# One core, two layers: where an image's tables are made, how a scan starts, and how a layer's beginning is cut up

## The chip, the core and the metric

The kernel runs on one core of a Trainium2 chip. The core has five engines with instruction queues of their own: TensorE (PE in the profile; PEld is its weight load), VectorE (DVE), ScalarE (ACT), GpSimd (POOL) and SyncE (SP), which here only issues DMAs. Each engine works through its queue in order and waits on semaphores for the others. The metric is the device time of one execution in microseconds (us), the median of several.

## The reference

The input `x` has 4 images of 128 x 128 pixels with 128 channels in float32. Two layers follow one another, each on a group-normalized input and each with a residual sum:

```
x = x + L0(gn(x))     # deformable convolution: per pixel 9 offsets, bilinear samples, depthwise 3x3, pointwise
x = x + L1(gn(x))     # two Mamba blocks over each image row (128 tokens)
```

What matters of the first layer is its sampling, from four neighbours of a fractional place:

```
out = wa * gather(y0, x0) + wb * gather(y1, x0) + wc * gather(y0, x1) + wd * gather(y1, x1)
```

and of the second, its selective scan, whose state has 16 numbers for each of 256 inner channels:

```
delta  = softplus(dt @ dtw + dtb)
h      = exp(delta * A) * h + (delta * u) * B      # one token after another
y      = sum over states of h * C   (+ u * D)
```

## The kernel before

**First layer (`layer0(b)`).** A work item is a unit `(j, u)`: four image rows `j` of 32 (`NJ`), and one of nine pairs of taps (`UNITS`). `gather` (L353) issues eight indirect DMAs per unit on POOL; each fetches, for 128 pixels by an index each, one row of a table in DRAM. The table of an image is made by `table_part(b, j)` (L207) from the normalized image, four rows at a time. Its row `e` has 2 x 128 numbers: for the pixel and for its neighbour to the right, the 64 channels of the pixel and of the one below it. So one index brings all four neighbours (1024 B). DVE normalizes (`xt` times `row_s`, plus `row_b`), SP issues eight writes a part: two channel groups, the pixel and its right neighbour, the upper and the lower row. Ahead of it, `stats_part(b, j)` (L181) loads four rows, transposes them on PE and takes their statistics on DVE, and `norm_part(b)` makes scale and bias of an image. `sample` (L373) multiplies what was gathered by the weights (`gw`, L382, on DVE), adds it up transposed on PE (`p`), and copies it with ACT to `s`; `add_up` (L399) runs the depthwise and pointwise products on PE. Gathered tiles have four buffers (`NGT`), two of which are a unit. `prep` makes indices and weights for eight rows.

Within `layer0(b)` stands a list `todo` (L428): the 32 statistics parts, the normalization and the 32 table parts of image `b + 1`, spread over the units of image `b`, three to each four rows. Image 0's own are made ahead of everything.

**Second layer (`layer1`).** A job is four image rows and one of two blocks; there are 256 jobs, 64 for each image, in the order: two row groups through block 0, the same two through block 1. `pre` (L484) begins a job: input products (`pu`, `pr`, L501 and L513), Silu for `u` and `g` on ACT, the small product `pdb` with its copy `dbl`, from which SP stores `bcd` to DRAM, then the softplus for `delta`: Abs, Exp, +1 and Ln on ACT (L538 to L546) and four half operations and two whole ones on DVE (L547 to L550: `e`, `de`, `du`). `main` (L553) has eight steps (`q`), two states each. In a step, SP loads B and C for it spread over all partitions (`bc`, two buffers each), ACT writes `da = exp(delta * A)` in four pieces (L580) into one of three `da` buffers, and DVE runs three operations of 128 x 2048: `hs` (L586, two instructions), the scan (L592), which overwrites `da` with the state, and the product with C (L596). PE then adds the result up transposed in PSUM (`y`, L128). After eight steps DVE multiplies `y` by the gate (`g`, L607), PE transposes and multiplies by the output weights, and ACT copies; in block 1 the result goes out from a tile `ot`.

All products are written as `scalar_tensor_tensor` with a column of `ones` as their scalar; the scan takes its initial value from a column `zero`.

**The order.** The program first makes image 0's statistics and table, then runs `layer0(0)` alone. Then it runs `layer1` over all images, and beside image `b`'s 512 steps the units of `layer0(b + 1)`, spread so that they end 24 steps early. Image 3's second layer has nothing beside it. In `layer1`, `pre` of the next job is written out whole ahead of `main` of the present one. The layer that turns the program into queues moves instructions within each engine's queue, so the built order is not that of the text; ACT's table loads (ACT_TABLE_LOAD) are put in where the function set changes.

Of the kernel before, what the change touches and what calls it, by code (L numbers as in the profile page):

```python
# [10 lines left out]
F32 = mybir.dt.float32  # L11
# [6 lines left out]
P = 128  # L18
G = 2
# [44 lines left out]
def block_kernel(ctx: ExitStack, tc: tile.TileContext, a: dict, out: bass.AP):  # L64
# [71 lines left out]
    dwb = loadw("dwb", [P, NT], pool=p2, tag="ot")  # L136
# [21 lines left out]
    dpar = loadw("dpar", [P, NL, NC], pool=p2, tag="ot")  # L158
# [32 lines left out]
    def norm_part(b):  # L191

        scale, bias = group_norm(nc, small, ps, stats[b], gavg, 1e-5, f"a{b}")
        rows = []
        for nm, v in (("s", scale), ("b", bias)):
            dg = small.tile([P, P], F32, tag="dg", name=f"dg_{nm}_{b}")
            nc.vector.tensor_scalar(dg, ident, v, None, ALU.mult)
            pr = ps.tile([P, 512], F32, tag="t", name=f"prow_{nm}_{b}")
            nc.tensor.matmul(pr[:, 0:P], ones, dg, start=True, stop=True)
            row = small.tile([P, P], F32, tag=f"row_{nm}", name=f"row_{nm}_{b}")  # L200
            nc.scalar.copy(row, pr[:, 0:P])
            rows.append(row)
        norm[b] = (scale, bias, rows[0], rows[1])
# [3 lines left out]
    def table_part(b, j):  # L207
        if j == 0:
            table[b] = dram.tile([G * (H - 1) * W, 2, 2 * CG], F32, name=f"table_{b}")
# [6 lines left out]
        nc.vector.tensor_tensor(xv, xv, brow.unsqueeze(1).to_broadcast([P, n + 1, P]), ALU.add)  # L216
        for g in range(G):

            e0 = (g * (H - 1) + 4 * j) * W
            for sx in range(2):  # L220

                parts = [(0, n, 0)] if e0 or not sx else [(0, 1, 1), (1, n - 1, 0)]
                for r, m, p0 in parts:
                    e = e0 + r * W - sx
                    tv = table[b][e + p0 : e + m * W, sx]
                    if p0 == 0:
                        tv = tv.rearrange("(r w) e -> w r e", w=W)
                    else:
                        tv = tv.unsqueeze(1)
                    for sy in range(2):  # L230
                        nc.sync.dma_start(
                            tv[:, :, CG * sy : CG * sy + CG],
                            xt[p0:, r + sy : r + sy + m, CG * g : CG * g + CG],
                        )
# [118 lines left out]
    def gather(b, j, u):  # L353

        wt, idx = locs[b, j // 2]
        flat = table[b][0 : G * (H - 1) * W - 1].rearrange("n s e -> n (s e)")
# [69 lines left out]
    def layer0(b):  # L426

        todo = []  # L428
        if b + 1 < B:
            todo += [lambda j=j: stats_part(b + 1, j) for j in range(NJ)]  # L430
            todo += [lambda: norm_part(b + 1)]
            todo += [lambda j=j: table_part(b + 1, j) for j in range(NJ)]
# [50 lines left out]

    def pre(st, l):  # L484
# [25 lines left out]
        for i in range(SR // 2):  # L510
# [7 lines left out]
            tc.keep_in_program_order(nc.scalar.activation(g[:, 2 * i : 2 * i + 2], px, AF.Silu))  # L518
        pdb = ps1.tile([P, TB], F32, tag="t", name=f"pdb_{nm}")
# [6 lines left out]
        nc.sync.dma_start(bcd, dbl[DTR + 1 : XP, :])  # L526

# [3 lines left out]
        es, pdts = [], []  # L531
        for c in range(NC):
# [4 lines left out]
            e = p2.tile([P, TB], F32, tag="e", name=f"e_{nm}_{c}", bufs=2)  # L537
            nc.scalar.activation(e, pdt, AF.Abs)  # L538
            nc.scalar.activation(e, e, AF.Exp, scale=-1.0)
            es.append(e)  # L540
            pdts.append(pdt)
        for c in range(NC):
            e = es[c]
            w1 = p2.tile([P, TB], F32, tag="w1", name=f"w1_{nm}_{c}")
            nc.scalar.activation(w1, e, AF.Identity, bias=1.0)
            nc.scalar.activation(du[:, c], w1, AF.Ln)  # L546
            nc.vector.scalar_tensor_tensor(e, w1, 1.0, e, op0=ALU.subtract, op1=ALU.subtract)  # L547
            nc.vector.scalar_tensor_tensor(de[:, c], pdts[c], 0.0, e, op0=ALU.max, op1=ALU.subtract)  # L548
# [4 lines left out]
    def main(st, l):  # L553
# [11 lines left out]
        for q in range(NS // NQ):  # L565
# [10 lines left out]
            for c in range(NC):  # L576
                dv = st["delta"][:, c].rearrange("p (s t) -> p s t", s=SR)
                for n in range(NQ):
# [3 lines left out]
                    )  # L582
            hs = p2.tile([P, NC, NQ, TB], F32, tag="hs", name=f"hs_{nm}_{q}")

            for n in range(NQ):
                nc.vector.scalar_tensor_tensor(  # L586
                    hs[:, :, n, :], st["du"], ones[:, 0:1],
                    bc[0][:, n].unsqueeze(1).to_broadcast([P, NC, TB]),
                    op0=ALU.mult, op1=ALU.mult,
                )  # L590
            df = da.rearrange("p c n s t -> p (c n s t)")
            nc.vector.tensor_tensor_scan(  # L592
                df, df, hs.rearrange("p c n t -> p (c n t)"), zero[:, 0:1], ALU.mult, ALU.add
            )
            dc = da.rearrange("p c n s t -> p c (n s t)")
            nc.vector.scalar_tensor_tensor(  # L596
                dc, dc, ones[:, 0:1],
                bc[1].rearrange("p n t -> p (n t)").unsqueeze(1).to_broadcast([P, NC, NQ * TB]),
                op0=ALU.mult, op1=ALU.mult,
            )  # L600
# [19 lines left out]
        else:  # L620
# [8 lines left out]
            ot = p2.tile([P, SR, P], F32, tag="ot", name=f"ot_{nm}")  # L629
# [11 lines left out]
    def layer1():  # L641
        pre(*jobs[0])
        for i, job in enumerate(jobs):
            if i + 1 < len(jobs):
                pre(*jobs[i + 1])
            yield from main(*job)
# [101 lines left out]
```

## Time and profile before

| what | value |
| --- | --- |
| time, median of 3 runs | 26681.26 us (26681.15 to 26698.94) |
| the profiled execution | 26698.06 us, span 26696.0 us |
| busy: PE / DVE / ACT / POOL | 19620.5 / 23505.8 / 11605.1 / 16017.0 us |
| share of the span: PE / DVE / ACT / POOL | 73 / 88 / 43 / 60% |
| mean granted TensorE clock | 0.845 |
| indirect gathers (POOL) | 9216, mean 1738 ns |
| ACT_TABLE_LOAD before `da` (L580) / before Ln (L546) | 1016 / 500, 1283 ns each |

Busy time is time in which the engine executed an instruction; waits, and the issue of DMAs, are not counted. A group line of the profile names the source line, the engine, the operation, what it writes and reads with shapes, its count, then busy time and the mean of one, and after the second bar how long the engine stood idle just before these instructions and what ended that. A list of waits gives who waited for whom: total us, times, longest. A timeline line has the start, the duration, and in brackets the idle time before it. The 40-slice view gives the busy share in tenths.

### The profile page before, as it was taken

The page shows a single profiled execution, that of the slowest core. Times are in us where ns is not written, and L with a number is a line of the kernel's source. Part 1 is how long each engine was busy: PE and PEld are TensorE (multiplying, and loading weights), DVE is VectorE, ACT ScalarE, POOL GpSimd, SP SyncE. Part 2 cuts the span into 40 slices and gives each one's busy share as a digit, 9 for nine tenths or more (in the row PEclk, how much of TensorE's full clock was granted, in tenths as well). Part 3 has the DMA queues.
Part 4 walks back from the last instruction along what each step waited for, and adds up shares of the span by engine and source line. Part 5 has one row for each costly group of instructions (what it writes and reads, how often), then busy time and mean ns, then how long its engine had stood idle before and what let it go on. Part 6 is the DMA issues. An engine that isn't in the chain of part 4 may idle for free. (4 is left out here: it accounts for less than half of the span.)

```text
span 26696.0 us, 294801 instructions
## 1 busy us (share of the span) xinstructions
PE 19620.5 (73%) x112196; PEld 13523.4 (51%) x112196; DVE 23505.8 (88%) x14042; ACT 11605.1 (43%) x18181; POOL 16017.0 (60%) x9222
## 2 busy tenths in 40 slices
PE   4777788878888778887888778888888655555555
PEld 3444455555555555555555555555555443434344
DVE  2232289999999999999999999999999999999999
ACT  0000044444444544444444454444445455555554
POOL 4777777878877767888878667877878400000000
PEclk7888888888999888888998888899998866666666
DMA  5363344456544444455544444444444333333332
GB/s 146 114 172 107 106 147 155 157 170 183 165 153 154 149 144 155 158 173 181 164 154 153 148 143 151 156 150 152 154 154 156 130 107 106 107 106 107 107 106 102
DMA packets 1994602, 3804.53 MB, mean 143 GB/s; under 512 B 771796, under 2 KB 1116116, under 8 KB 1993053
## 3 DMA queue, kind: packets, MB, share of 16 engines
q1 hardware_dynamic: 1550812, 2577.13, 29.9%
q0 software_dynamic: 442368, 1208.55, 14.4%
q8 instruction: 880, 14.42, 0.2%
q14 instruction: 542, 4.43, 0.0%
HBM read 3567.63 MB, written 217.05 MB: 142 GB/s over the span
## 5 line engine op out<-in xcount | busy, mean ns | idle before, releaser
L364 POOL DMA_INDIRECT gt<-table,idx x9216 | 16016.3, 1738 | 5031.5 <-issue 2999.5
L592 DVE TENSOR_TENSOR_SCAN da<-da,zero,hs 128x2048 f32<-128x2048 f32 x2048 | 9176.1, 4481 | 351.7 <-ACT da L580 247.1
L128 PE MATMUL y<-ident,da 128*128 128x128 f32 x32768 | 5252.0, 326 | 3956.1 <-DVE da L596 3955.4
L580 ACT ACTIVATE da<-de,aneg 128x508 f32<-128x508 f32 x8192 | 5550.5, 712 | 5605.2 <-PE y L128 5351.0
L128 PEld LDWEIGHTS y<-ident,da 128*128 128x128 f32 x32768 | 4682.4, 171 | 4953.3 <-DVE da L596 2520.6
L415 PE MATMUL acc<-s,wc 128*64 128x256 f32 (+3 forms) x38400 | 6403.2, 453 | 761.4 <-ACT s L396 760.9
L586 DVE SCALAR_TENSOR_TENSOR hs<-du,ones,bc 128x1024 f32<-128x1024 f32 x4096 | 5093.2, 1277 | 0.0
L415 PEld LDWEIGHTS acc<-s,wc 128*64 128x64 f32 x38400 | 3352.0, 145 | 3083.2 <-issue 1446.2
L596 DVE SCALAR_TENSOR_TENSOR da<-da,ones,bc 128x2048 f32<-128x2048 f32 x2048 | 4807.9, 2348 | 25.9
L382 DVE TENSOR_TENSOR gw<-gt,wt 128x1024 f32<-128x1024 f32 x2304 | 2786.4, 1213 | 2133.3 <-DMA gt<-table,idx 1500.9
L128 PE MATMUL p<-ident,gw 128*128 128x128 f32 x18432 | 2724.3, 299 | 1714.1 <-DVE gw L382 1706.7
L128 PEld LDWEIGHTS p<-ident,gw 128*128 128x128 f32 x18432 | 2292.8, 154 | 2329.3 <-DVE gw L382 1752.7
L396 ACT COPY s<-p 128x512 f32<-128x512 f32 x1152 | 668.6, 581 | 3989.8 <-PE p L128 3982.0
L501 PE MATMUL pu<-hp,inc 128*128 128x512 f32 x4096 | 1808.3, 593 | 0.0
L580 ACT ACT_TABLE_LOAD x1016 | 1303.5, 1283 | 16.8 <-PE y L128 5.7
L501 PEld LDWEIGHTS pu<-hp,inc 128*128 128x128 f32 x4096 | 751.2, 188 | 865.9 <-issue 865.2
L508 ACT ACTIVATE u<-pu,w_cvb 128x512 f32<-128x512 f32 x512 | 324.6, 684 | 1468.9 <-PE y L561 1461.4
L561 PEld LDWEIGHTS y<-ddiag,u 128*128 128x128 f32 x4096 | 579.5, 200 | 192.0 <-issue 192.0
L612 PE MATMUL pyg<-ident,g 128*128 128x128 f32 x2048 | 353.9, 328 | 425.7 <-DVE g L607 424.8
L546 ACT ACT_TABLE_LOAD x500 | 641.5, 1283 | 8.9
L561 PE MATMUL y<-ddiag,u 128*128 128x128 f32 x4096 | 612.1, 284 | 0.0
L263 PE MATMUL pof<-xn,w_offw 128*64 128x512 f32 x2304 | 585.0, 613 | 20.0 <-ACT xn L257 12.0
(118 smaller groups left out, 11036.3 us busy)
## 6 DMA issues: line engine op xcount, KB each, us to landing
bc<-bcd SPq DMA_DIRECT2D x4096, 512.0 KB
gt<-table,idx POOLq DMA_INDIRECT x9216
table<-xt SPq DMA_DIRECT2D x984, 128.0 KB
xt<-in_x SPq DMA_DIRECT2D x124, 320.0 KB
xr<-in_x SPq DMA_DIRECT2D x128, 256.0 KB
x<-xo SPq DMA_DIRECT2D x128, 256.0 KB
x1t<-x SPq DMA_DIRECT2D x128, 256.0 KB
x1t_o<-x SPq DMA_DIRECT2D x128, 256.0 KB
```

The costliest lines, as they stand in the source:

```text
L128: nc.tensor.matmul(o, v, ident, is_transpose=True, start=start, stop=stop, skip_group_check=True)
L364: nc.gpsimd.indirect_dma_start(out=gt[:, v, r], out_offset=None, in_=flat, in_offset=bass.IndirectOffsetOnAxis(ap=idx[:, ri, o : o + 1], a ...
L382: nc.vector.tensor_tensor(gw.rearrange("p r s v c -> p (r s) v c"), gts[h].rearrange("p v r (s c) -> p (r s) v c", c=CG), wv.unsqueeze(3). ...
L396: nc.scalar.copy(st[:, :, 1 : W + 1], p4)
L415: nc.tensor.matmul(accs[b, j + i0][CG * g : CG * g + CG, q : q + rb - ra, :], wc[sl, v, e, :], st[p + 4 * g if p < 4 else 8][sl, ra:rb, kx ...
L501: nc.tensor.matmul(px.rearrange("p (s t) -> p s t", s=SR), inc[:, l, j, c * P : (c + 1) * P], h[:, :, j : j + P], start=(j == 0), stop=(j ...
L546: nc.scalar.activation(du[:, c], w1, AF.Ln)
L561: nc.tensor.matmul(y[:, i, c], st["u"][:, c, i * P : (i + 1) * P], ddiag[:, l, c, :], start=(i % 2 == 0 and c == 0), stop=False, skip_grou ...
L580: nc.scalar.activation(da[:, c, n, :, 1:], dv[:, :, 1:], AF.Exp, scale=aneg[:, l, c, s : s + 1])
L586: nc.vector.scalar_tensor_tensor(hs[:, :, n, :], st["du"], ones[:, 0:1], bc[0][:, n].unsqueeze(1).to_broadcast([P, NC, TB]), op0=ALU.mult, ...
L592: nc.vector.tensor_tensor_scan(df, df, hs.rearrange("p c n t -> p (c n t)"), zero[:, 0:1], ALU.mult, ALU.add)
L596: nc.vector.scalar_tensor_tensor(dc, dc, ones[:, 0:1], bc[1].rearrange("p n t -> p (n t)").unsqueeze(1).to_broadcast([P, NC, NQ * TB]), op ...
```

## The change

The change has five parts.

1. `todo` is filled in `layer0(0)` alone, with the statistics, normalization and tables of images 1, 2 and 3: 195 items, seven to each four rows, where each `layer0(b)` had 65 for the next image.
2. A table row has half the size: the pixel and the one below it, for 64 channels. One index still fetches 256 numbers, which are now two rows in succession, the pixel and its right neighbour. The sums go into a new tile `xg`, laid out by channel group, with one buffer; SP issues eight writes a part, one for each row and group.
3. The scan's initial value is the constant 0.0.
4. In the last image's jobs `hs` and the product with C are plain `tensor_tensor` operations, `hs` as one instruction in place of two.
5. `pre` is a generator with four stops. `main` advances it once per step, so the next job's beginning is written out in pieces behind the first five steps. In it, the softplus works on whole 128 x 1024 tiles: ACT takes the maximum (Relu) and subtracts 1, and DVE has four whole operations.

Some tiles change their tag, so that the memory suffices: `ot` shares with `w1`, and the diagonal matrices of the normalization share with `wn`.

```diff
     def table_part(b, j):
         if j == 0:
-            table[b] = dram.tile([G * (H - 1) * W, 2, 2 * CG], F32, name=f"table_{b}")
+            table[b] = dram.tile([G * (H - 1) * W, 2 * CG], F32, name=f"table_{b}")
...
         nc.vector.tensor_tensor(xv, xv, srow.unsqueeze(1).to_broadcast([P, n + 1, P]), ALU.mult)
-        nc.vector.tensor_tensor(xv, xv, brow.unsqueeze(1).to_broadcast([P, n + 1, P]), ALU.add)
+
+        xg = pb.tile([P, G, 5, CG], F32, tag="xg", name=f"xg_{b}_{j}", bufs=1)
         for g in range(G):
...
+            c = slice(CG * g, CG * g + CG)
+            nc.vector.tensor_tensor(
+                xg[:, g, 0 : n + 1], xv[:, :, c], brow[:, c].unsqueeze(1).to_broadcast([P, n + 1, CG]), ALU.add
+            )
+        for g in range(G):
             e0 = (g * (H - 1) + 4 * j) * W
...
+            for r in range(n):
+                nc.sync.dma_start(
+                    table[b][e0 + r * W : e0 + r * W + W], xg[:, g, r : r + 2].rearrange("p r c -> p (r c)")
+                )
...
-        flat = table[b][0 : G * (H - 1) * W - 1].rearrange("n s e -> n (s e)")
+
+        flat = table[b][:]
...
-        if b + 1 < B:
-            todo += [lambda j=j: stats_part(b + 1, j) for j in range(NJ)]
-            todo += [lambda: norm_part(b + 1)]
-            todo += [lambda j=j: table_part(b + 1, j) for j in range(NJ)]
+        for i in range(1, B) if b == 0 else ():
+            todo += [lambda i=i, j=j: stats_part(i, j) for j in range(NJ)]
+            todo += [lambda i=i: norm_part(i)]
+            todo += [lambda i=i, j=j: table_part(i, j) for j in range(NJ)]
...
+        yield
         pdb = ps1.tile([P, TB], F32, tag="t", name=f"pdb_{nm}")
...
         nc.sync.dma_start(bcd, dbl[DTR + 1 : XP, :])
+        yield
...
-            nc.scalar.activation(e, pdt, AF.Abs)
-            nc.scalar.activation(e, e, AF.Exp, scale=-1.0)
...
-        for c in range(NC):
-            e = es[c]
-            w1 = p2.tile([P, TB], F32, tag="w1", name=f"w1_{nm}_{c}")
-            nc.scalar.activation(w1, e, AF.Identity, bias=1.0)
-            nc.scalar.activation(du[:, c], w1, AF.Ln)
-            nc.vector.scalar_tensor_tensor(e, w1, 1.0, e, op0=ALU.subtract, op1=ALU.subtract)
-            nc.vector.scalar_tensor_tensor(de[:, c], pdts[c], 0.0, e, op0=ALU.max, op1=ALU.subtract)
+            nc.scalar.activation(e[:, c], pdt, AF.Abs)
+            nc.scalar.activation(de[:, c], pdt, AF.Relu)
+        nc.scalar.activation(e, e, AF.Exp, scale=-1.0)
+        nc.scalar.activation(w1, e, AF.Identity, bias=1.0)
+        nc.scalar.activation(du, w1, AF.Ln)
+        nc.scalar.activation(w1, w1, AF.Identity, bias=-1.0)
+        yield
+        yield
+        nc.vector.tensor_tensor(e, w1, e, ALU.subtract)
+        nc.vector.tensor_tensor(de, de, e, ALU.subtract)
         nc.vector.tensor_tensor(de, de, du, ALU.add)
...
+            if in_last(blk):
+                nc.vector.tensor_tensor(
+                    hs,
+                    st["du"].unsqueeze(2).to_broadcast([P, NC, NQ, TB]),
+                    bc[0].unsqueeze(1).to_broadcast([P, NC, NQ, TB]),
+                    ALU.mult,
                 )
...
-                df, df, hs.rearrange("p c n t -> p (c n t)"), zero[:, 0:1], ALU.mult, ALU.add
-            )
...
+                df, df, hs.rearrange("p c n t -> p (c n t)"), 0.0, ALU.mult, ALU.add
+            )
+            if in_last(blk):
+                nc.vector.tensor_tensor(dc, dc, cv, ALU.mult)
+            else:
+                nc.vector.scalar_tensor_tensor(dc, dc, ones[:, 0:1], cv, op0=ALU.mult, op1=ALU.mult)
...
     def layer1():
-        pre(*jobs[0])
+        for _ in pre(*jobs[0]):
+            pass
         for i, job in enumerate(jobs):
-            if i + 1 < len(jobs):
-                pre(*jobs[i + 1])
-            yield from main(*job)
+
+            nxt = pre(*jobs[i + 1]) if i + 1 < len(jobs) else iter(())
+            for _ in main(*job):
+                next(nxt, None)
+                yield
+            for _ in nxt:
+                pass
```

## The prediction

> **What bounds the kernel now.** I read first the page's 40 slices, then busy time by stage, then the groups of VectorE (DVE), what it waits for, and the timeline of single steps.
>
> ```profile
> PE   4777788878888778887888778888888655555555
> DVE  2232289999999999999999999999999999999999
> POOL 4777777878877767888878667877878400000000
> ...
> 330.00:1330.00 1000.00, 792.90 (x4989) 494.38 (x4989) 276.08 (x315) 76.16 (x133) 773.47 (x744) 0.88 0.39 114
> 1345.00:2345.00 1000.00, 795.70 (x4918) 478.51 (x4914) 309.32 (x368) 75.75 (x135) 774.87 (x740) 0.88 0.55 150
> 2400.00:3400.00 1000.00, 788.10 (x4893) 472.35 (x4893) 257.38 (x280) 76.22 (x134) 772.12 (x749) 0.88 0.36 106
> 3436.00:21354.00 17918.00, 14309.54 (x83937) 9846.38 (x83937) 17474.17 (x10407) 8668.91 (x13655) 13606.18 (x6898) 0.89 0.48 156
> 21354.00:26696.00 5342.00, 2791.45 (x12672) 2140.90 (x12672) 5061.15 (x2489) 2691.71 (x4093) 0.00 (x0) 0.69 0.31 106
> ```
>
> Columns of the stretches: length, then busy time of PE, weight load, DVE, ACT, POOL. There are three stages. To 3436 image 0's first layer runs alone; DVE is a quarter busy, and POOL issues one gather per 1000/749 = 1.335 us without waiting for anything but itself: POOL is the bound. The three stretches there hold image 1's statistics (744 gathers), its table (740) and neither (749). From 3436 to 21354 DVE is 97.5% busy (second layer of images 0 to 2 beside the first layer of images 1 to 3). From 21354 POOL is idle and the second layer of image 3 runs alone: 64 jobs in 5342 us, 83.5 us each, DVE 94.7% busy.
>
> ```profile
> L592 DVE TENSOR_TENSOR_SCAN da<-da,zero,hs 128x2048 f32<-128x2048 f32 x2048 | 9176.1, 4481 | 351.7 <-ACT da L580 247.1 <-PE pdt L534 11.2 <-DVE hs L586 3.3
> L586 DVE SCALAR_TENSOR_TENSOR hs<-du,ones,bc 128x1024 f32<-128x1024 f32 x4096 | 5093.2, 1277 | 0.0
> L596 DVE SCALAR_TENSOR_TENSOR da<-da,ones,bc 128x2048 f32<-128x2048 f32 x2048 | 4807.9, 2348 | 25.9
> L549 DVE TENSOR_TENSOR de<-de,du 128x1024 f32<-128x1024 f32 x256 | 311.3, 1216 | 1.4 <-ACT du L546 1.2
> L607 DVE TENSOR_TENSOR g<-y,g 128x1024 f32<-128x1024 f32 x256 | 310.9, 1214 | 110.1 <-PE y L128 109.7
> L303 DVE TENSOR_TENSOR wn<-loc,fl 128x288 f32<-128x288 f32 x64 | 29.0, 452 | 0.0
> L304 DVE SCALAR_TENSOR_TENSOR wn<-loc,wn 128x288 f32<-128x288 f32 x64 | 28.9, 452 | 0.0
> ...
> 23159.36 4.49 DVE L592 TENSOR_TENSOR_SCAN da<-da,zero,hs 128x2048 f32<-128x2048 f32 x1
> 23163.88 2.35 DVE L596 SCALAR_TENSOR_TENSOR da<-da,ones,bc 128x2048 f32<-128x2048 f32 x1
> 23166.15 2.48 DVE L586 SCALAR_TENSOR_TENSOR hs<-du,ones,bc 128x1024 f32<-128x1024 f32 x2
> 23168.76 4.49 DVE L592 TENSOR_TENSOR_SCAN da<-da,zero,hs 128x2048 f32<-128x2048 f32 x1
> ...
> DVE da L592 <- ACT da L580: 196.3, 62, 5.6
> ```
>
> A step in the last image is three DVE operations back to back, scan to scan 9.40 us. The last row is the last image's one wait of size: 62 times in 64 jobs the scan waits for ACT's `da`. The timeline puts it at the third scan behind a job's start: ACT is then at the next job's beginning, switching tables (1.28 us a load, eight a job) and standing for PE, between the `da` of one step.
>
> **The change, part by part**, summed against the profiled execution, 26698.06 us (2 us more than its span).
>
> *Constant scan initial.* A `[P,1]` operand has a price in these rows: 1277 ns with `ones` against 1216 without at 128x1024, while L304, with a constant for its scalar, takes the 452 of the plain L303. I take the same 0.06 us off each scan. The scan with a constant isn't in the trace: bounds 0 and -0.06. 2048 x 0.06 = **-123 us**, all on DVE; 512 of them are in the last image, 1536 before.
>
> *Plain products in the last image.* 1024 more elements cost 2348 - 1277 = 1071 ns, so a plain product of 2048 takes about 1216 + 1071 = 2287 ns. The pair of `hs` (2.48 us) becomes one of 2.29, the `da` product goes from 2.35 to 2.29: 0.25 x 512 = **-128 us**. POOL, which such products could hold up, does nothing there.
>
> *The delta chain.* Per job DVE has now four half operations (0.60 us from start to start, L547 and L548) and two of 128x1024 (1.12): 4.62 us with the shorter first one. Four of 1.12 are 4.48: 256 x 0.14 = **-36 us**. ACT takes over the maximum (a Relu per half) and the -1 (one pass), some 2 us a job, and drops table loads: 2036 to 1040 in the built order, 996 x 1.283 = 1278 us. ACT is 50% busy in the last image, so this counts only through waits.
>
> *The layer in pieces: waits that go.* In the built order ACT does all four `da` of a step before the next job's first Silu, then both Silu pairs under one load, and Exp and Ln under one load each. By the durations above, the `da` of the third step after a job's start is then done some 10 us ahead of its scan, where it is now up to 5.6 late. So I take out 196 + 11 us (last image), and in the stretch before, the 51 us of the same wait and 20 of L547 for L545: **-278 us**; bounds 0 and that.
>
> *A wait that comes.* `g` (L607) reads the last transposes of the job before, which PE ends 3.83 us after DVE's last product (the trace's last `g` waits so long with nothing in between). Now in the last image scan and `hs` stand ahead of it, and it doesn't wait. In the changed order 47 of 64 times only the one `hs` product (2.2 us) does: 47 x 1.6 = 75 us. Before the last image `g` stands right behind the `hs` pair 117 times where it was 69; at 106 us for 76 waits, 1.4 each, 48 more are 67 us. Behind `g` waits the scan, and all of DVE. **+142 us**; bounds 40 and 180.
>
> *Statistics and tables of images 2 and 3 out of the DVE-bound stretch.* There, 64 statistics (44 us), 128 products and sums of the table (103), small ones (2); less 0.08 us overlap each (15), plus 10 of waiting for PE: **-144 us**. Their DMAs leave too: 64 x (8 table writes + 1 load) and 64 loads on SP. The busy share of DVE is 98.4% between 11000 and 13000, where a table is written, 97.7% between 7000 and 9000, where less is, so I give nothing for them.
>
> *The same work in stage 0.* Seven items per four rows now, not three. A statistics part cost (749 - 744) x 1.335 / 31 = 0.2 us of POOL's pace, a table part (749 - 740) x 1.335 / 31 = 0.4: 64 x 0.2 + 64 x 0.45 = 42 us (the sum is now two operations). A table part issues 8 writes of 64 KB in 512 B rows, where it was 8 of 128 KB in 256 B rows, behind one another on SP with the next part's load, and ahead of image 0's loads; DMA is busy 0.55 there, so bandwidth is no bound. But `xg` has one buffer: the sums of a part wait until the 8 writes of the part before have landed, about 8 x 0.5 + 2 us, and the `gw` products of the gathers stand behind them on DVE. In the built order this falls on every second part; `gw` has about 4 us of waiting for its gather per half unit to hide it in, and four gather buffers keep POOL going. I take 33 us for what isn't hidden: **+75 us**, bounds +20 and +250. Image 0's own table, before any gather, keeps its pace: SP's 16 issues take 9.0 of 14.4 us per two parts now, and the single buffer makes a chain of the same length (within 30 us either way).
>
> The port that both engines need is where a page bears on this.
>
> ```profile
> 12008.06 4.03 POOL L364 DMA_INDIRECT gt<-table,idx  x1 [0.31 <-issue]
> 12006.85 4.47 DVE L592 TENSOR_TENSOR_SCAN da<-da,zero,hs 128x2048 f32<-128x2048 f32 x1
> ```
>
> A gather that takes 0.95 us alone took 4.03 and ended 0.77 us after the scan beside it. The Trainium skill (GPSIMD Engine Reference, § Specifications) says that POOL's path to SBUF contends with DVE instructions that have two SBUF inputs. That speaks against moving tables into the one stage that POOL bounds: by the rule each added table operation could hold a gather for all its length, where the counts above gave 0.4 us a part. It is the second rival.
>
> **Sum**: -123 - 128 - 36 - 278 + 142 - 144 + 75 = -492, so 26,206 for an execution like the profiled one. The median shown, 26,681.26, lies 17 us lower; I predict **26,200 us**.
>
> **Rivals.**
>
> 1. *A gather becomes two rows: slower.* The table's row is now 512 B, and one index fetches 1024 B, two rows. If POOL wrote a descriptor per table row, its 0.95 us would double at most: stage 0 alone gets 2304 x 0.95 = 2190 us longer, 28,400; the point from which it decides is 492 / 2304 = 0.21 us per gather. For it: no gather in the trace fetches past its row. Against: the destination stays one run of 1024 B, and the built instruction names 256 elements per index as before. Chance 0.07.
> 2. *POOL held in full.* 64 parts x (0.81 + 2 x 0.48) of table operations hold gathers for their whole length: 113 us, 84 more than my 29: 26,290. For it the 4.03 us above; against it the count of gathers. 0.07.
> 3. *The pieces free nothing.* The waits for `da` move to another step, because Relu and the -1 come into the same queue: 278 stay, 26,480. For it: PE's order puts the products of the next job's beginning ahead of the transposes; against: eight loads become four. 0.10.
> 4. *Single `xg`.* If DVE's standing on the writes reaches POOL at each of 96 parts with 2.5 us: +240 in place of 33, 26,410. For it: every part's sums wait on all 8 writes; against: four gather buffers. 0.08.
> 5. *Gains and losses cancel* within 0.2%, some 53 us, about what a measurement of this kernel tells from no change. 0.04.
>
> **How the numbers follow.** The forecast has 0.64. It, POOL held, the pieces and `xg` all end faster: 0.89. Same 0.04, slower 0.07. Range: best, with +20 in stage 0, +40 for `g` and 30 off the first table, the sum is -679, so 26,019; I take 26,030, since the ends hardly all come together. Above, 26,450 holds all of rivals 2 and 4 and nearly reaches 3. The forecast's own range is 26,060 to 26,340.
>
> **What would show it.** Scan 4.42 us; last image: one `hs` product of 2.29, scan to scan 9.07, a job about 79.5; `da` from ACT gone from DVE's waits there, `g` for PE come in its place with about 1.6 us each; DVE's stretch before it shorter by some 300 us; stage 0 ending near 3510 in place of 3436, with POOL's gathers at 1.37 to 1.39 us apart. Gathers above 1.5 us would be rival 1; `xg` waiting for table DMAs beside POOL waiting for `gw` would be rival 4.

## The result, and the profile after

The changed kernel takes **26059.91 us** (median of 4 runs, 26054.35 to 26064.71) where the kernel before takes 26685.15 on the same chip: a ratio of 0.9765, 95% interval 0.9748 to 0.9782, or 625 us less. The prediction said 26,200 with a range of 26,030 to 26,450. It lies inside, 140 us too high.

The groups of the profile after that answer to those shown of before, from the page (line, engine, operation, tiles and count, then busy time, mean ns of one, idle time before):

```profile
L603 DVE TENSOR_TENSOR_SCAN da<-da,hs 128x2048 f32<-128x2048 f32 x2048 | 9049.6, 4419 | 108.4 <-DVE hs L597 2.3
L607 DVE TENSOR_TENSOR da<-da,bc 128x2048 f32<-128x2048 f32 x512 | 1172.6, 2290 | 14.3
L587 DVE TENSOR_TENSOR hs<-du,bc 128x2048 f32<-128x2048 f32 x512 | 1169.5, 2284 | 0.0
```

A scan with a constant initial takes 4419 ns where it took 4481; the plain products take 2284 and 2290 ns; ACT's `da` no longer stands among what the scan waits for. The working's unit prices for these three are confirmed to the hundredth of a microsecond. A job of the last image takes 79.3 us (5075.5 / 64, from 20980.9 on) where some 79.5 were forecast.

To see where the time came from, I cut both executions at two instants that are easy to find in any of these traces: the start of the first scan (the end of stage 0) and the start of the last product with gathered data (`gw`, the end of the first layers).

| kernel | first gather | stage 0 (to the first scan) | middle | last part | span |
| --- | --- | --- | --- | --- | --- |
| before | 319.7 | 3471.2 | 17594.2 | 5630.6 | 26696.0 |
| changed | 275.7 | 3429.0 | 17265.7 | 5361.7 | 26056.4 |
| difference | -44.0 | -42.2 | -328.5 | -268.9 | -639.6 |
| the prediction's terms | 0 | +75 | -267 | -300 | -492 |

The last row sorts the terms on record by stage: middle 1536 x 0.06 + 192 x 0.14 + 71 - 67 + 144 = 267, last part 31 + 128 + 9 + 207 - 75 = 300. The terms took the last image for the last part, which holds some 3.5 jobs more. So two stages came out near their sums, one 61 better and one 31 worse, and stage 0 came out 117 better.

The same cut in busy time by stretch (length; then PE, weight load, DVE, ACT, POOL):

```profile
3429.00:20694.70 17265.70, 13940.06 (x82728) 9563.39 (x82724) 16947.89 (x9650) 7820.08 (x12659) 13573.22 (x6880) 0.89 0.47 154
20694.70:26056.00 5361.30, 2978.07 (x13475) 2258.89 (x13473) 5196.26 (x1996) 2589.43 (x4061) 0.00 (x0) 0.70 0.33 111
```

DVE is 98.2% busy in the middle and 96.9% in the last part: it remains the bound, and what is left idle is 318 and 165 us. Half of the latter is one kind of wait. The last image's waits of DVE, and the timeline around one of them:

```profile
DVE g L616 <- PE y L128: 78.8, 48, 3.8
DVE e L547 <- ACT w L544: 10.1, 36, 0.3
```

```profile
23109.42 4.42 DVE L603 TENSOR_TENSOR_SCAN da<-da,hs 128x2048 f32<-128x2048 f32 x1
23113.88 2.29 DVE L607 TENSOR_TENSOR da<-da,bc 128x2048 f32<-128x2048 f32 x1
23116.08 2.29 DVE L587 TENSOR_TENSOR hs<-du,bc 128x2048 f32<-128x2048 f32 x1
23119.99 1.23 DVE L616 TENSOR_TENSOR g<-y,g 128x1024 f32<-128x1024 f32 x1 [1.62 <-PE y L128]
23121.14 4.41 DVE L603 TENSOR_TENSOR_SCAN da<-da,hs 128x2048 f32<-128x2048 f32 x1
```

The `da` wait of before (196.3 us, 62 times) is gone entirely. In its place `g` waits 48 times for PE's transposes, 1.6 us each: the last product of a job (L607) ends at 23116.17, only one `hs` stands between, and `g` is next in the queue before PE is done. Behind it waits the scan.

In stage 0 the chain is POOL's. Its gathers keep their pace: 1040 ns each from the first gather to the end of the stage in both kernels, and that stretch is 3151 us before and 3153 after although 128 more items run beside it. What DVE waits for between the first gather and the end of the stage, before and after:

```profile
DVE gw L382 <- DMA gt<-table,idx: 1388.8, 393, 16.7
DVE gw L382 <- PE p L128: 604.3, 113, 15.6
```

```profile
DVE gw L377 <- DMA gt<-table,idx: 1388.2, 408, 11.3
DVE gw L377 <- PE p L128: 272.1, 64, 7.4
DVE xg L220 <- DMA table<-xg: 167.5, 46, 6.5
```

DVE does wait for `xg`'s writes, as rival 4 had it, but that doesn't lengthen the stage: `gw` waiting for PE falls from 604.3 to 272.1 us.

### The profile page after: what moved, and what is told of

Same layout as the page of the kernel before. It is cut to its first block, busy times and chain, and to the rows that moved or that the text cites. A ratio compares the mean times of both kernels' runs of the same rounds, so it can differ in the third digit from the quotient of the medians.

```text
span 26056.4 us, 293200 instructions
## 1 busy us (share of the span) xinstructions
PE 19489.8 (75%) x112196; PEld 13423.5 (52%) x112196; DVE 23278.6 (89%) x13146; ACT 10677.0 (41%) x17185; POOL 16003.4 (61%) x9222
## 5 line engine op out<-in xcount | busy, mean ns | idle before, releaser
L603 DVE TENSOR_TENSOR_SCAN da<-da,hs 128x2048 f32<-128x2048 f32 x2048 | 9049.6, 4419 | 108.4 <-DVE hs L597 2.3
L410 PE MATMUL acc<-s,wc 128*64 128x256 f32 (+3 forms) x38400 | 6153.9, 446 | 346.9 <-ACT s L391 345.1
L597 DVE SCALAR_TENSOR_TENSOR hs<-du,ones,bc 128x1024 f32<-128x1024 f32 x3072 | 3829.9, 1280 | 0.0
L609 DVE SCALAR_TENSOR_TENSOR da<-da,ones,bc 128x2048 f32<-128x2048 f32 x1536 | 3605.0, 2347 | 18.2
L607 DVE TENSOR_TENSOR da<-da,bc 128x2048 f32<-128x2048 f32 x512 | 1172.6, 2290 | 14.3
L587 DVE TENSOR_TENSOR hs<-du,bc 128x2048 f32<-128x2048 f32 x512 | 1169.5, 2284 | 0.0
L575 ACT COPY da<-zero 128x16 f32<-128x16 f32 x2048 | 426.1, 208 | 719.5 <-PE y L128 679.7
L536 PE MATMUL pdt<-dbl,w_dtw 9*128 9x512 f32 x1024 | 578.9, 684 | 2.0 <-ACT dbl L524 2.0
```

The lines of the kernel that those rows point to most:

```text
L410: nc.tensor.matmul(accs[b, j + i0][CG * g : CG * g + CG, q : q + rb - ra, :], wc[sl, v, e, :], st[p + 4 * g if p < 4 else 8][sl, ra:rb, kx ...
L587: nc.vector.tensor_tensor(hs, st["du"].unsqueeze(2).to_broadcast([P, NC, NQ, TB]), bc[0].unsqueeze(1).to_broadcast([P, NC, NQ, TB]), ALU.mult,
L597: nc.vector.scalar_tensor_tensor(hs[:, :, n, :], st["du"], ones[:, 0:1], bc[0][:, n].unsqueeze(1).to_broadcast([P, NC, TB]), op0=ALU.mult, ...
L603: nc.vector.tensor_tensor_scan(df, df, hs.rearrange("p c n t -> p (c n t)"), 0.0, ALU.mult, ALU.add)
L607: nc.vector.tensor_tensor(dc, dc, cv, ALU.mult)
L609: nc.vector.scalar_tensor_tensor(dc, dc, ones[:, 0:1], cv, op0=ALU.mult, op1=ALU.mult)
```

## The experiments

Five undo a part of the change or half of one (part 5 in two runs), one overloads stage 0, and four try what else the trace seems to offer, one of them twice. No run undoes part 2, the smaller table row, by itself. "Longer" is against 26061.05 us, the changed kernel run again (`r_after`) beside a kernel before of 26696.62; beside the first four that undo something, before took 26695.22, so the times can be put side by side.

**The yardstick.** The changed kernel unaltered:

> The changed kernel again, unaltered, as the yardstick for the three runs beside it and for whether its ratio to the kernel before depends on the chip. If the gain lies in VectorE's queue (middle stretch and last image), it is 600 to 640 us on any chip and the ratio lies between 0.975 and 0.978; if it depends on how fast the memory answers, the ratio moves with the length of stage 0.

26061.05 us, ratio 0.9764 (0.9747 to 0.978). Its stages are 3433.2, 17266.0 and 5362.0: within 5 us of the first profile.

**Tables beside each image, as before** (one part undone):

```
-        for i in range(1, B) if b == 0 else ():
+        for i in range(b + 1, min(b + 2, B)):
```

> The changed kernel with one part undone: each image's first layer makes the statistics and table of the next image, as before; all else as changed. Theory (work moved out of a DVE-bound stretch, free where it went): stage 0 keeps its length, 3118 us from the first gather to the second layer's start, within 15; the stretch after it, 17,588 us in the changed kernel, gets longer by the DVE work of 64 statistics and table parts, 64 x (0.69 + 0.82 + 2 x 0.49) = 159 less 20 of overlap plus 10 of waits, so about +150 in all, 26,210. Rival A (the table's DMAs and SP's queue also held up the gathers, of whose waits some 100 us went): +250, with DVE's waits for gathers back near 110 us. Rival B (POOL did pay in stage 0): stage 0 shorter by 40 and more, +110 or less.

26149.62 us, ratio 0.9799 (0.9782 to 0.9815): 89 us longer. By the profile the middle is 17354.6, 89 longer, and stage 0 is 3422.5, 7 to 11 shorter than in the two profiles of the changed kernel. From the first gather to the first scan it takes 3147.6 us here and 3151.9 to 3168.2 in seven profiles whose stage 0 has all three images' items (those of the four kernels further below that ran on a slower chip are left out), so 128 items cost stage 0 some 10 us, between 4 and 21. Rival A falls with DVE's waits for gathers (50.0 us in the middle, 55.4 in the yardstick), and rival B with the small gain in stage 0; the theory's place is right and its 150 too much. Busy time of the middle, and three rows of DVE's groups in it:

```profile
3422.50:20777.10 17354.60, 14004.73 (x83034) 9651.37 (x83032) 17064.08 (x9923) 7842.09 (x12675) 13674.75 (x6880) 0.89 0.49 157
...
L220 DVE TENSOR_TENSOR xg<-xt,row_b 128x320 f32<-128x320 f32 (+1 forms) x128 | 59.8, 467 | 0.0
L215 DVE TENSOR_TENSOR xt<-xt,row_s 128x640 f32<-128x640 f32 x64 | 51.3, 801 | 0.0
L189 DVE BATCH_NORM_STATS2 stats<-pt 128x6 f32<-128x512 f32 x64 | 43.8, 685 | 5.2 <-PE pt L188 5.2
```

DVE is busy 116 us longer (17064 against 16948), and its idle time is 291 instead of 318: part of the work filled time in which DVE otherwise waited. So 144 was too much.

**The pieces taken out** (the next job's beginning whole, ahead of the present one):

```
-            for _ in main(*job):
-                next(nxt, None)
-                yield
             for _ in nxt:
                 pass
+            yield from main(*job)
```

> The changed kernel with the next job's beginning written out whole ahead of the present job's steps, as before; the softplus on whole tiles stays. Theory (the pieces removed the scan's wait for ACT): the last image's scans wait about 200 us for ACT again, the stretch before some 50, and the 79 us of g's wait in the last image go, so +120 to +250. Rival (what removed the waits is the softplus with one table load for Exp and one for Ln and no DVE steps between ACT's): under +60, waits of the scan for ACT under 80 us.

26285.66 us, ratio 0.9848 (0.9831 to 0.9864): 225 longer, 61 in the middle and 158 in the last part. DVE's waits in the last part:

```profile
DVE da L603 <- ACT da L580: 200.1, 66, 4.6
DVE e L547 <- ACT w L544: 71.2, 66, 1.1
DVE g L616 <- PE y L128: 3.8, 1, 3.8
```

The wait for `da` is back as it was (196.3 before), and `e` waits for the softplus 66 times (10 us in the changed kernel). `g` doesn't wait. In the middle the waits for gathers are 131.9 against 55.4. The rival's under 60 is refuted: the softplus on whole tiles alone doesn't free the scan. But ACT's table loads rise too, from 1040 to 1542 in all, so this run doesn't tell the order in pieces from the smaller number of loads that comes with it.

**The scan's initial from a tensor again:**

```
-                df, df, hs.rearrange("p c n t -> p (c n t)"), 0.0, ALU.mult, ALU.add
+                df, df, hs.rearrange("p c n t -> p (c n t)"), zero[:, 0:1], ALU.mult, ALU.add
```

> The changed kernel with the scan's initial value read from the column again. Theory (DVE sets the end in both later stages): 4481 ns a scan in place of 4419, 2048 x 0.062 = +127 us. Rival (only the last image, where nothing but DVE works, passes it on): 512 x 0.062 = +32 us, the rest going into other waits of DVE.

26164.02 us, ratio 0.9803 (0.9787 to 0.982): 103 longer; the scan is 4481 ns again. The last part is 5393.4, 31 longer; 540 scans start in it, which makes 540 x 0.062 = 33. The middle is 61 longer where the other 1508 would make 93: DVE is busy 91 us longer there (17036.9 against 16946.2) and idle 30 less, since it has waits that a longer scan fills (`g` for PE 131.0 instead of 145.2, among others). So the theory holds but for these 30.

**The last image's products with `ones` again:**

```
     def in_last(blk):
-        return blk * SR // H == B - 1
+        return False
```

> The changed kernel with scalar_tensor_tensor and the pair for hs in the last image too. Theory (operation for operation): 512 x (0.196 + 0.058) = +130 us. Rival (the pair gives PE the time that g now waits for): g's 79 us of waiting in the last image go down to under 20, so +70 or less.

26117.31 us, ratio 0.9787 (0.9771 to 0.9803): 56 longer, 47 of it in the last part, though DVE is busy 125 us longer there (5321.6 against 5196.2). So the rival holds. A job's end in the last image:

```profile
23147.26 2.48 DVE L597 SCALAR_TENSOR_TENSOR hs<-du,ones,bc 128x1024 f32<-128x1024 f32 x2
23149.87 4.42 DVE L603 TENSOR_TENSOR_SCAN da<-da,hs 128x2048 f32<-128x2048 f32 x1
23154.22 1.20 DVE L616 TENSOR_TENSOR g<-y,g 128x1024 f32<-128x1024 f32 x1
23155.33 2.34 DVE L609 SCALAR_TENSOR_TENSOR da<-da,ones,bc 128x2048 f32<-128x2048 f32 x1
```

Here the built queue has `g` behind the scan, not ahead of it, and it waits for nothing: the 79 us of waiting are gone, and the 10 of `e`. DVE is idle 87.6 us in the last part instead of 165.8, and 125 - 78 = 47. So the wait of `g` in the last image isn't the price of the pieces alone: it needs both them and the plain products, since either one undone puts `g` at another place in the queue.

**The delta chain by halves, as before:**

```
-            nc.scalar.activation(de[:, c], pdt, AF.Relu)
-        nc.scalar.activation(e, e, AF.Exp, scale=-1.0)
...
+            nc.scalar.activation(e[:, c], e[:, c], AF.Exp, scale=-1.0)
+            pdts.append(pdt)
+        for c in range(NC):
+            nc.scalar.activation(w1[:, c], e[:, c], AF.Identity, bias=1.0)
+            nc.scalar.activation(du[:, c], w1[:, c], AF.Ln)
...
-        nc.vector.tensor_tensor(e, w1, e, ALU.subtract)
-        nc.vector.tensor_tensor(de, de, e, ALU.subtract)
+        for c in range(NC):
+            nc.vector.scalar_tensor_tensor(e[:, c], w1[:, c], 1.0, e[:, c], op0=ALU.subtract, op1=ALU.subtract)
+            nc.vector.scalar_tensor_tensor(de[:, c], pdts[c], 0.0, e[:, c], op0=ALU.max, op1=ALU.subtract)
```

> The delta chain per half as before the change (Abs and Exp by halves, + 1 and Ln by halves, the maximum and the - 1 in VectorE's two scalar_tensor_tensor per half), everything else as changed. Theory: the order in pieces alone took the da waits away, and the chain is worth its own VectorE time, 36 to 75 us longer than the changed kernel. Rival: the halved number of table loads on ACT is what freed the scan; with some 500 loads of 1.28 us back, the scan waits for da again and it is 150 to 250 us longer.

26163.43 us, ratio 0.9803 (0.9786 to 0.9819): 102 longer, more than the theory's 75 and less than the rival's 150. The rival couldn't show itself: the table loads did not come back (540 before `da`, 518 in the changed kernel, 1016 before), since the built order grouped most of the halves by itself; and the scan hardly waits for `da` (2.0 us). Rows of the middle:

```profile
L377 DVE TENSOR_TENSOR gw<-gt,wt 128x1024 f32<-128x1024 f32 x1718 | 2070.7, 1208 | 188.6 <-DMA gt<-table,idx 157.1 <-PE y L128 18.8 <-PE p L128 12.3
L550 DVE SCALAR_TENSOR_TENSOR de<-pdt,e 128x512 f32<-128x512 f32 x376 | 250.8, 676 | 0.0
L549 DVE SCALAR_TENSOR_TENSOR e<-w,e 128x512 f32<-128x512 f32 x375 | 250.7, 677 | 0.0
```

By their own durations the four halves are 46 us more there than the two whole operations (250.8 + 250.7 against 227.9 + 227.3), but they overlap: DVE's busy time in the middle grows by 26 us. Its idle time grows by 91, and it waits 157 us for gathers instead of 49 to 55. These 100 us are what the prediction had no term for. They fall at a job's end (126 of the 157 us come after the seventh or eighth scan behind `g`, 38 of 55 in the yardstick). Why gathers come later there isn't shown. The last image by itself, from its first scan on, is no longer than in the yardstick (5072.8 against 5073.4 us): there the whole tiles bring nothing.

**Every statistics and table part of images 1 to 3 twice:**

```
-        if j == 0:
+        if b not in table:
...
-            todo += [lambda i=i, j=j: stats_part(i, j) for j in range(NJ)]
+            todo += [lambda i=i, j=j: stats_part(i, j) for j in range(NJ) for _ in range(2)]
...
-            todo += [lambda i=i, j=j: table_part(i, j) for j in range(NJ)]
+            todo += [lambda i=i, j=j: table_part(i, j) for j in range(NJ) for _ in range(2)]
```

> Every statistics part and every table part of images 1 to 3 is done twice beside image 0's first layer (the same values written twice): 192 more items in stage 0. If that stage's length is set by POOL's gathers alone and VectorE's waits for them hide the items, stage 0 is no longer than in the changed kernel, within 30 us, and the whole is the same. By the prediction's prices (0.2 us of POOL's pace a statistics part, 0.4 to 0.5 a table part, and some not hidden of the single xg) it would be 75 us for 128 items, so 110 or more for these 192. If the queue of SP or xg is full, several hundred.

26141.19 us, ratio 0.9793 (0.9777 to 0.9809): 80 longer, 74 of it in stage 0 (3507.5 against 3433.2), the rest as in the yardstick. Neither number was right: 192 more items are not free, and they cost less than 110. POOL in stage 0, first the yardstick, then the doubled kernel:

```profile
L359 POOL DMA_INDIRECT gt<-table,idx x2336 | 2432.2, 1041 | 999.2 <-issue 683.7 <-DMA table<-xg 273.4 <-DVE gw L377 15.6
```

```profile
L359 POOL DMA_INDIRECT gt<-table,idx x2336 | 2479.6, 1061 | 1026.2 <-issue 673.1 <-DMA table<-xg 275.0 <-DVE gw L377 34.8
```

Of the 74, 47 are longer gathers (1061 against 1041 ns), and 19 are POOL waiting for `gw`. So it is 74 / 192 = 0.39 us an item, near the price that I had put on a table part, where the first 128 items got by with 10 / 128 = 0.08. DVE had not run out of waiting: it still waits 1137.3 us for gathers in stage 0, 1390.0 in the yardstick. What grows is what it holds up. Counted over the records, the gathers of stage 0 that take over 1.0 us and end 0.7 to 0.9 us behind a product or sum of a table are 24 in the kernel with each image's table apart, 84 in the yardstick and 164 here; beyond 0.95 us each they take 9, 25 and 49 us. `gw` holds 495 in the yardstick and 442 here, for 186 and 214 us.

**Plain products in all images.** Does what pays in the last image pay everywhere? `in_last` returns True; in a second kernel the `hs` product stays in two of 1024 as well. These two ran with the next two on another chip, where before took 27374.31 us and stage 0 of all four kernels is 690 to 730 us longer (first scan at 4121 to 4164); the later stages are not (17260.8 and 5364.4 in the last of them, where the change is untouched), so I read these by stage.

> The changed kernel with plain products in all images, hs as one instruction of 128x2048 everywhere. Theory (scalar_tensor_tensor with two tiles holds POOL's gathers just as a plain product does, so the form is of no matter to POOL): 1536 x 0.25 = 384 us less DVE work in the middle stretch, of which g's wait for PE and the missing gap between the pair take some 100: 25,700 to 25,850, gathers in that stretch at the same mean, 1970 ns. Rival (plain products hold up POOL more, which is why they stand in the last image alone): gathers in that stretch longer by 100 ns and more, DVE waiting for gathers by several hundred us: 26,060 or slower.

> The same with hs as two plain products of 128x1024, also in the last image. Theory: 2048 x (0.06 x 2 + 0.06) for the columns, which is 1536 x 0.18 = 277 us less in the middle stretch, and 512 x 0.07 = 36 us more in the last image: about 25,820; the gap between the pair lets a gather in as now. Rival (it is the gap between the pair and not the form that POOL needs): n_plain slower than this one, by 100 us and more, with longer gathers. Rival (the plain form): 26,060 or slower, like n_plain.

28235.24 us, ratio 1.0314 (1.0297 to 1.0331), and 28138.26 us, ratio 1.0279 (1.0262 to 1.0296): slower than before. Both theories fell, and the rival of the plain form holds in both; as a pair the products give back 97 us. The middle is 18724.4 and 18623.0, some 1460 and 1360 us longer than with `ones` on that chip, while each product is shorter by 0.06 us. Gathers there take 2378 and 2338 ns in the mean, against 1985 on the same chip with the `ones` products. The two timelines show how. First the kernel with `ones` (DVE, then POOL), then plain products everywhere:

```profile
12020.20 2.35 DVE L609 SCALAR_TENSOR_TENSOR da<-da,ones,bc 128x2048 f32<-128x2048 f32 x1
12022.47 2.47 DVE L597 SCALAR_TENSOR_TENSOR hs<-du,ones,bc 128x1024 f32<-128x1024 f32 x2
...
12020.22 0.95 POOL L359 DMA_INDIRECT gt<-table,idx  x1 [0.30 <-issue]
12021.47 1.89 POOL L359 DMA_INDIRECT gt<-table,idx  x1 [0.30 <-issue]
12023.67 0.94 POOL L359 DMA_INDIRECT gt<-table,idx  x1 [0.30 <-issue]
```

```profile
12024.06 2.28 DVE L587 TENSOR_TENSOR hs<-du,bc 128x2048 f32<-128x2048 f32 x1
12026.26 1.22 DVE L549 TENSOR_TENSOR de<-de,du 128x1024 f32<-128x1024 f32 x1
...
12024.13 3.04 POOL L359 DMA_INDIRECT gt<-table,idx  x1 [0.30 <-issue]
```

A gather that begins within some 0.1 us of the start of a `ones` product passes in 0.95 us (the one at 12020.22). One that begins later in it is held and ends 0.8 us after it (12021.47 + 1.89 is 0.81 past the end at 12022.55). Beside a plain product also the one that begins with it is held: 12024.13 + 3.04 is 0.83 past the end of L587 at 12026.34. Counted over the records between 5 and 20 ms, the changed kernel against plain products everywhere:

```
gather begins in the first tenth of the product    count    under 1.1 us    median us
da product with ones (2.35 us)                      652        100%           0.95
da product, plain    (2.29 us)                      530          2%           3.08
hs product, plain    (2.28 us)                      169          1%           3.03
```

The `hs` products with `ones`, 1.28 us each, let one gather through each: of 1200 that begin in their first 0.15 us, 99% take 0.95. Gathers that begin beyond the first tenth and before the middle of a product are held by both forms. Of the 652, 650 begin within 0.08 us of the product's start and pass; the earliest one held begins 0.22 us in, so the opening ends somewhere between. All 119 gathers that begin beside `g`, a plain product with one of its two inputs in PSUM, take 0.95 us in the changed kernel. DVE then waits for gathers 1721.7 us in the middle where plain products stand, 64.0 with `ones`.

**`g` pinned behind the next job's first scan.** If `g`'s wait is one of place in the queue, moving it is worth what it waits:

```
+            if q == 0:
+                if tails:
+                    tails.pop()()
+                y = begin()
...
+            if q == NS // NQ - 1:
+                tails.append(lambda: tail(st, l, y))
...
-        nc.vector.tensor_tensor(gt, y.rearrange("p s c d -> p s (c d)"), gt, ALU.mult)
+        tc.keep_in_program_order(
+            nc.vector.tensor_tensor(gt, y.rearrange("p s c d -> p s (c d)"), gt, ALU.mult)
+        )
```

(`begin` is the opening of `y`'s sums, `tail` all from `g` on.)

> The changed kernel with the gate's product g of a job held behind the first scan of the next job on DVE. Theory (g stands too early and holds up DVE until PE's transposes end): the 226 us that DVE waits for PE in front of g go, nothing takes their place, so -150 to -226: 25,840 to 25,910. Rival (PE, ACT and the next beginning then come later by a scan, 4.4 us a job, and DVE waits for them instead): within 60 us of the changed kernel.

26538.70 us, ratio 0.9695 (0.9678 to 0.9711); middle 17118.4, last part 5258.7, 147 and 103 less than the changed kernel on the yardstick's chip. That is more than the 226 us that `g` waits, so both guesses were too low. Beside the yardstick, on its chip:

> The late g once more beside the changed kernel on the same chip: the tail of a layer (g and what follows) pinned behind the first scan of the next. If g's wait for PE (226 us in the changed kernel) is all there is to be had, it is 210 to 250 us shorter than the changed kernel, the gain split some 145 in the middle stretch and some 100 in the last image. If the earlier difference was that of the chips, it is within 60 us of it.

25814.74 us, ratio 0.9672 (0.9656 to 0.9688): 246 less than the changed kernel, the fastest of all, within the 210 to 250; middle 17121.5, last part 5258.3. DVE's idle time falls by 147 us in the middle and by 86 in the last part. A job's end in it:

```profile
23089.82 4.42 DVE L607 TENSOR_TENSOR_SCAN da<-da,hs 128x2048 f32<-128x2048 f32 x1
23094.16 1.20 DVE L632 TENSOR_TENSOR g<-y,g 128x1024 f32<-128x1024 f32 x1
23095.28 2.28 DVE L615 TENSOR_TENSOR da<-da,bc 128x2048 f32<-128x2048 f32 x1
```

**Two `xg` buffers while image 0's table is made.** The second is lent by `gw`, which isn't used yet:

```
-        xg = pb.tile([P, G, 5, CG], F32, tag="xg", name=f"xg_{b}_{j}", bufs=1)
+        xg = pb.tile([P, G, 5, CG], F32, tag="xg" if b else "gw", name=f"xg_{b}_{j}", bufs=1 if b else 2)
```

> The changed kernel with two buffers for xg while image 0's table is made (in the memory of gw, which is idle then). Theory (the first table's pace of 5.5 us a part is SP's eight issues, 3.6 us, plus waiting for the one buffer): 4.1 to 4.5 us a part, so the first gather starts 30 to 45 us earlier and the whole ends as much earlier, about 26,020. Rival (landing of the writes or loads bounds it): within 10 us.

26784.28 us, ratio 0.9782 (0.9766 to 0.9798). The expectation fell: the first gather starts at 289.3, 14 us later than on that chip without the edit (275.0), not earlier. SP's queue in the changed kernel, then in this one (with one row of DVE):

```profile
201.89 0.43 SPq L214 DMA_DIRECT2D xt<-in_x  x1
203.79 3.64 SPq L226 DMA_DIRECT2D table<-xg  x8
207.47 0.43 SPq L214 DMA_DIRECT2D xt<-in_x  x1
209.27 3.65 SPq L226 DMA_DIRECT2D table<-xg  x8
```

```profile
200.29 1.00 SPq L214 DMA_DIRECT2D xt<-in_x  x2
203.83 0.82 DVE L215 TENSOR_TENSOR xt<-xt,row_s 128x640 f32<-128x640 f32 x1 [9.00 <-DMA xt<-in_x]
205.20 7.45 SPq L226 DMA_DIRECT2D table<-xg  x16
212.70 1.00 SPq L214 DMA_DIRECT2D xt<-in_x  x2
```

With one buffer a part goes round in 5.5 us; with two, the parts go in pairs, 12.4 us for two, and the pair's sums wait 9.0 us for loads that were issued behind sixteen writes. Before the change it was pairs too, at 14.4 us. So the single buffer, which I had feared, is what gives each load its place between the writes. It also divides the 44 us: with the new writes still in pairs the first gather starts at 289.3, 30 earlier than before the change, and the other 14 come with the single parts.

## Why the prediction came out as it did

- **The bound, and what a microsecond of DVE is worth: right.** In the middle DVE's busy time fell by 239 us and its idle time by 90, in the last part by 139 and 130. The undone parts come near the whole: 89 + 225 + 103 + 56 + 102 = 575 us, with the 44 of image 0's table 619, where the change brought 636 on the yardstick's chip. It is no clean sum: two of the runs free the same 75 us of `g`'s wait in the last image, and no run undoes part 2 alone.
- **Scan: price right, size a little high.** 62 ns a scan as predicted; -123 was forecast, 103 came back when undone. In the middle a third of it fills time in which DVE waits.
- **Plain products and the `g` wait: right together.** -128 + 75 = -53 forecast, 56 measured (47 of it in the last part); 48 waits of 1.6 us where 47 were forecast. The wait was booked under the pieces; the runs show that it hangs on the products as well.
- **The pieces: right in mechanism.** -278 + 142 = -136 was forecast. The scan's waits for `da` and `pdt` went from 258 us to none; the 20 of `e` were not saved (22 after, outside stage 0). `g`'s waits rose by 117, from 110 to 226. That makes -141, near the forecast. Undone, the pieces are worth more, 225: `da` comes back with 230 us, `e` with 81, and gathers come late by 76 more in the middle, for which the prediction had no term; `g` gives back 126. That sums to 261; smaller waits and DVE's work make up the difference. Rival 3, that the waits would only move, is refuted: 196 us to none in the last image. Whether the order or the halved table loads did it was not separated.
- **The delta chain: mis-sized.** -36 forecast, 102 measured. The term counted DVE's operations, which the 26 us of busy time in the middle bear out; it left out the waits for gathers, which make up most of it.
- **Statistics and tables out of the middle: -144 forecast, 89 measured.** DVE has 116 us less to do; 27 of it had been hidden in waits.
- **The middle's sum: partly luck.** -267 forecast, -328.5 measured. The 55 us too much for statistics and tables, the 75 too little for the delta chain there and the gathers' waits without a term partly cancel.
- **The same work in stage 0: the step that failed.** "**+75 us**" stood for what the items would cost there, 33 of it for the single `xg`. They cost about 10, with POOL's gathers 1.350 us apart, 1.346 before, where 1.37 to 1.39 were to be seen. DVE did the items in time in which it waits for gathers and PE, and few gathers were held by them. A price of 0.2 to 0.45 us an item is what the next 192 cost, as the doubled kernel shows, not what the first ones cost; why the price rises is shown only so far as more and longer holds of gathers go with it. I took it from slices of stage 0 that differed by 5 and 9 gathers in 744, which was too little to tell a price from.
- **Image 0's table: the second step that failed.** "The single buffer makes a chain of the same length (within 30 us either way)" was 44 us off. Eight writes of the new form are issued in 3.64 us, 0.455 apiece; sixteen of the old form took 9.0, 0.56 apiece; and parts no longer go in pairs.
- **Rivals 1, 2 and 4 fell on one row.** Gathers of two table rows take the same 1040 ns in stage 0 as gathers of one (rival 1). Gathers held for the full length of the table operations would have shown in it: those behind table operations lost some 23 us, where rival 2 had 113. The Trainium skill (GPSIMD Engine Reference, § Specifications) says that POOL's SBUF interface contends with DVE instructions that have two SBUF inputs. The runs agree for plain products and for gathers that meet a `ones` product well under way, and differ for those that begin with one (99.7% against 2% unheld), though both forms have two such inputs. POOL waited 15.6 us for `gw` in the yardstick, not 240 (rival 4).

## What to carry to other kernels

Work moved out of the stage that an engine bounds into one in which the same engine waits can be nearly free: here 128 items cost about 10 us, and 192 more cost 74 though the engine still waited a good deal. So count the idle time that work can hide in before giving it a price per item, and what it holds up on the engine that bounds the stage. A shorter operation can cost its own gain where a queue is in order: look at which instruction now comes up early, and pin it behind something long (`g` behind the scan gave 246 us, more than any single part of the change was worth when undone). What pays where one engine is alone can lose where it shares with another: the same plain products gain in the last image and cost 1.4 ms beside gathers.

## What the runs showed of the hardware that I had not expected

- A `scalar_tensor_tensor` with a column of `ones` leaves an opening at its start in which a gather gets through (650 of 650 that begin in its first 0.08 us); a plain product of the same two tensors leaves next to none (2% of 530). The some 60 ns that the column costs DVE go with 1985 against 2378 ns a gather in the middle.
- Stage 0 was 690 to 730 us longer on one chip than on the others, in all four kernels run there, while middle and last part were alike to 5 us where the same code ran on both. DVE's waits for gathered data there (974 to 1041 us) end by something that the profile names only as remote. The cause stays open.
- SP's issue time hangs on the form of the DMA: 0.455 us for a write of the new form (64 KB in 512 B runs), 0.56 for one of the old (128 KB in 256 B runs). Size and run length were not separated.
